# One batch's output stored during the last attention, and two products first in the last output projection

## The chip, the cores and the metric

The kernel runs on one core of a Trainium2 chip. The metric is the time of one execution on the device in microseconds; where several runs are shown, their median counts. All data are float32 in memory. The engines are named PE (matrix products), DVE (VectorE), ACT (ScalarE), POOL (GpSimd) and SP (here it only issues DMAs). Each engine works through its own queue in order.

## The reference

Two blocks follow each other, each a group normalisation, an attention and an addition to the block's input. The input is 8 images of 32 x 32 positions and 512 channels, so 1024 tokens in each of 8 batches.

```python
def reference(x, w_qkv, w_proj, b_proj, Wq, Wk, Wv, Wo, pos_emb_w, pos_emb_h):
    # layer 0: 16 heads of 32
    x = x + attention(_gn(x); w_qkv) @ w_proj + b_proj
    # layer 1: 4 heads of 128
    q = _gn(x) @ Wq / sqrt(128); k = _gn(x) @ Wk; v = _gn(x) @ Wv
    scores = q @ k + relative_logits(q, pos_emb_w, pos_emb_h)
    x = x + softmax(scores) @ v @ Wo
    return x
```

Here `_gn` is a group normalisation over 32 groups of channels; heads, reshapes and the form of the relative logits are cut.

## The kernel before, in words

**Layout.** A batch's activations lie transposed in SBUF: channels on the 128 partitions, in four chunks, and the 1024 tokens along the free dimension. Such a tensor is a `block` of 128 x 4 x 1024; eight of them are there (`BLOCKS`).

**Products.** All projections go through `seven`, a product of 2 x 2 blocks done in seven half-size products in place of eight. The moving operand is split into four quarters by chunk (`:HC`, `HC:`) and by token half (`:NB`, `NB:`). `forms` makes three sums (`s1`, `s2`, `s4`) of them and replaces the quarter `a21` by `a11 - a21`: four additions on DVE of 128 x 1024 elements. The seven moving operands are numbered 0 to 6: 0 is `a11`, 1 is `a12`, 2 is `s4`, 3 is `a22`, 4 is `s1`, 5 is `s2`, 6 is the new `a21`. Operands 0 and 1 are parts of the tensor itself, of its first token half. `ORDER` says in which order they are multiplied. Three banks of PSUM (`x`, `y`, `z`, from a ring of three) take the sums. A snapshot `p1` of bank `x` is taken by ACT after product 0; `a` and `b` are bank `y` plus `p1`, taken by DVE before more is added to the bank, so PE has to wait for them; `p7` is a snapshot of `z` by ACT. A projection consists of two units (`u` = 0 and 1) of 128 output columns of each half.

One product is eight matmul instructions of 32 columns (`by_columns`), four groups of columns side by side; the profile shows two records for each instruction, so `x16`.

**Weights.** `Stream` loads the weight parts in the order of the whole program's `plan`: after each product it issues the load that is seven products ahead, as a DMA on SP's queue, into a ring of 16 buffers (tag `w`).

**Output projection.** `after_1(b)` fetches the batch's saved activations from memory into a block `x2T`, runs `forms` on the attention's output (earlier, by a hook, in most batches), and then the two units. Results are added to `x2T` by the class `Onto`: `gather` adds snapshots on POOL, `add` adds banks on DVE. After each finished 128 x 512 part `add` calls `put_out`: a transpose on DVE into a tile `ot` (tag `row`, a ring of three), and four DMAs of 64 KB to the output, in pieces of 128 bytes. They are issued on SP; in the last batch every second one on ACT.

**The second attention.** `attention_1` has 4 heads x 2 query halves x 8 key tiles = 64 steps. A step multiplies scores on PE, takes the exponential on ACT into `e` (a ring of three), multiplies `e` with the values on PE, and adds `e` to a running sum `esum` on DVE. After eight steps `finish` and `normalise` divide by the sum: PE, ACT, DVE and, at the end, one multiplication on POOL.

**Order of the work.** The loop over `b` weaves the parts of three batches by generators and counts of steps. A scheduler of the framework then places the instructions in each engine's queue, mostly in the order of the program text; `issue_after` ties an instruction behind another one. In the last pass (`b` = 8) no first attention is left. The pass is the first output projection of batch 7, the second output projection of batch 6 (`after_1(6)`) with the normalisation of batch 7 woven in, the projections of batch 7 (`second`), and its attention. Behind the loop stands

```python
    run(after_1(B - 1, states[B - 1]))
```

and after it a check of all sums: `worst`, `bad`, a matmul `pf`, and `flag`, which every engine loads and branches on.

Of the kernel before, what the change touches and what calls it, by code (L numbers as in the profile page):

```python
# [17 lines left out]
P = 128  # L18
# [9 lines left out]
def quick_path(  # L28
# [52 lines left out]
    def bank(name, shape=None):  # L81
        return psum.tile(shape or [P, NB], F32, tag="bank", name=name, bufs=3)
# [80 lines left out]


    ORDER = [0, 5, 1, 4, 6, 2, 3]

    class Stream:

# [2 lines left out]
        def __init__(self, plan):  # L171
            self.plan = plan
            self.tiles = {}
            self.at = -1
            for i in ORDER:
                self.load(0, i)

        def load(self, n, i):
            if n >= len(self.plan):
                return  # L180
            m, rows, u = self.plan[n]
            if rows and u == 1:
                self.tiles[n, i] = self.tiles[n - 1, i]
                return
            got = []
            src = m.factor(i)
            if m.kept:
                got = [src[:, c, :] if rows else src[:, c, u * P : (u + 1) * P] for c in range(HC)]
                if i == ORDER[-1] and (u == 1 or rows):
                    m.kept = None  # L190
            elif rows:
                for c in range(HC):
                    t = mem.tile([P, HN], F32, tag="w", name=f"w_{m.name}_{n}_{i}_{c}", bufs=16)
                    nc.sync.dma_start(t, src[:, c, :])
                    got.append(t)
            else:
                t = mem.tile([P, HC, P], F32, tag="w", name=f"w_{m.name}_{n}_{i}", bufs=16)
                nc.sync.dma_start(t, src[:, :, u * P : (u + 1) * P])
                got = [t[:, c, :] for c in range(HC)]
            self.tiles[n, i] = got  # L200

        def unit(self, m, rows, u):
            self.at += 1
            assert self.plan[self.at] == (m, rows, u)
# [5 lines left out]
        def ahead(self, i):  # L210
            self.load(self.at + 1, i)

    def put_away(xT, name):
        kept = []
# [88 lines left out]

    in_place = [False]

    half_done = [None]

    def by_columns(out, weights, moving, start, stop, open_sum=False):
# [32 lines left out]
    def seven(fs, u, rows, sink, name, hook=None):  # L341

        def product(out, i, start):
            w, f = stream.take(i), fs[i]
            if not rows:
                for c in range(HC):
                    by_columns(out, w[c], f[:, c, :], start and c == 0, c == HC - 1, True)  # L350
            else:
                for t in range(2):
                    for c in range(HC):
                        by_columns(
                            out[:, t * HN : (t + 1) * HN],
                            f[:, c, (2 * u + t) * P : (2 * u + t + 1) * P],
                            w[c],
                            start and c == 0 and t == 0,
                            c == HC - 1,
                            True,  # L360
                        )
            stream.ahead(i)
# [9 lines left out]
        nc.vector.tensor_add(a, y, p1)  # L372
# [12 lines left out]
        p7 = snapshot("e1", f"p7_{name}")  # L385
        nc.scalar.copy(p7, z)  # L386
        yield HC
        product(y, 2, False)
        sink.c12(y, p1)
        if hook is not None:  # L390
            hook()
        yield HC
        product(z, 3, False)
        sink.c21(z, a)
        sink.c22(b, p7)
        yield HC

    class Plain:

# [237 lines left out]
    def attention_1(q, k, v, posT, b):  # L637

        steps = [(h, c, j) for h in range(H1) for c in range(NH) for j in range(NT)]
        state = {}  # L640

        def front(h, c, j):
            name = f"1_{b}_{h}_{c}_{j}"
            ps = bank(f"ps_{name}")
            keys = slice(j * P, (j + 1) * P)
            queries = slice(c * NB, (c + 1) * NB)
            nc.tensor.matmul(ps, k[h][:, keys], q[:, h, queries], start=True, stop=False)  # L647
            nc.tensor.matmul(ps, sel_flat[:, keys], posT[:, h, queries], start=False, stop=True)  # L648
            e = mem.tile([P, NB], F32, tag="e1", name=f"e_{name}", bufs=3)
            nc.scalar.activation(e, ps, AF.Exp, scale=1.0 / math.sqrt(D1))  # L650
            return e

        def back(h, c, j, e):
            name = f"1_{b}_{h}_{c}_{j}"
            if j == 0:
                state["acc"] = bank(f"acc_{name}")
                state["first"] = e
            acc = state["acc"]
            nc.tensor.matmul(  # L659
                acc,  # L660
                v[:, j, h * D1 : (h + 1) * D1],
                e,
                start=(j == 0),
                stop=(j == NT - 1),
            )
            if j == 1:
                state["esum"] = mem.tile([P, NB], F32, tag="es1", name=f"es_{name}", bufs=2)
                nc.vector.tensor_add(state["esum"], state["first"], e)  # L668
            elif j > 1:
                nc.vector.tensor_add(state["esum"], state["esum"], e)  # L670
            if j < NT - 1:
                return
            nc.scalar.copy(q[:, h, c * NB : (c + 1) * NB], acc)
            state["ended"] = (h, c, state["esum"])

        def finish(h, c, esum):
            name = f"1_{b}_{h}_{c}"
            su = bank(f"sums_{name}")
            nc.tensor.matmul(su, ones, esum, start=True, stop=True)
            normalise(q[:, h, c * NB : (c + 1) * NB], su, name)  # L680

        pending = None
        for at in steps:
            e = front(*at)
            ended = state.pop("ended", None)
            if pending is not None:
                back(*pending)
            pending = (*at, e)
            if ended is not None:
# [133 lines left out]

    def after_1(b, st, hook=None):

        if "ao1" not in st:
            forms_1(b, st)
        fs = st.pop("ao1")
        xT = fetch(st["kept"], block(f"x2T_{b}"))
        for u in range(2):  # L830

            def put_out(n, h):
                m = n * HC + u
                ot = mem.tile([P, NB], F32, tag="row", name=f"ot_{b}_{m}_{h}", bufs=3)
                nc.vector.transpose(ot, xT[m][:, h * NB : (h + 1) * NB])
                ot = ot.rearrange("p (t i) -> p t i", i=32)
                for a in range(P // 32):

                    queue = nc.scalar if b == B - 1 and a % 2 else nc.sync
                    queue.dma_start(  # L840
                        by_blocks(of[b, h * NB : (h + 1) * NB, :], m * P + 32 * a),
                        ot[32 * a : 32 * a + 32],
                    )

            stream.unit(WO, False, u)
            yield from seven(
                fs, u, False, Onto(halves(xT, u), then=put_out), f"wo_{b}_{u}", hook if u else None
            )

    def woven(main, side, start, gap, places=(0,)):  # L850

# [45 lines left out]
    WP, WQ1, WK1 = Matrix(w_proj, 0, "p"), Matrix(Wq, 0, "q1"), Matrix(Wk, 0, "k1")  # L897
    WV1, WO = Matrix(Wv, 0, "v1"), Matrix(Wo, 0, "o")
    def units(m, rows=False):
        return [(m, rows, u) for u in range(2)]  # L900

    FIRST = units(WQ0) + units(WK0) + units(WV0, True)
    plan = units(WV0, True) + [(m, False, u) for u in range(2) for m in (WQ0, WK0)]
    for b in range(B + 1):
        if b >= 1:
            plan += units(WP)
# [3 lines left out]
            plan += units(WQ1) + units(WK1) + units(WV1, True)  # L910
        if b + 1 < B:
            plan += FIRST
    plan += units(WO)

    states = [{} for _ in range(B)]
    load_first(states[0])
# [19 lines left out]
    for b in range(B + 1):  # L936
# [11 lines left out]
        if last is not None:  # L948
# [12 lines left out]
            if here is not None and coming is None:  # L961
# [5 lines left out]
                    H1 * NH * NT,  # L967
                )
                total += H1 * NT
            rest.append(woven(attention, incoming, 4, 6))  # L970
        else:
            rest.append(woven(rest_of_first(here), incoming, 0, 2))
# [503 lines left out]
```

## Time and profile before

| what | value |
|---|---|
| median of 5 runs | 3889.31 us (3886.48 to 3891.76) |
| profiled execution, its own time | 3885.46 us |
| its span, first to last instruction | 3883.7 us |
| PE busy | 3803.0 us, 98% |
| DVE busy | 2513.5 us, 65% |
| ACT busy | 1724.3 us, 44% |
| POOL busy | 620.4 us, 16% |
| granted PE clock, mean | 0.995 |
| second output projection of batch 6, first product | 3596.6 us from the start |
| attention of batch 7, first scores | 3711.3 us |
| last output projection, first product | 3843.0 us |
| last DVE instruction (a transpose of outputs) ends | 3875.7 us |

All places in the text are microseconds from the start of the span. A row of the timeline gives start, length, engine, line, operation, output and inputs with partitions x elements, and how many instructions are merged; in brackets stands the engine's idle time before it and what ended it. `SPq` and `ACTq` rows are DMA issues on those queues. The `p`, `f_ao` or `w_q` of a row are the program's tile names without numbers.

### The profile page before, as it was taken

The numbers are of one execution on the slowest core, as the hardware profiler recorded it, in microseconds if no ns is written. First come the engines' busy times: TensorE is split into PE (matmuls) and PEld (weight loads), VectorE is DVE, ScalarE is ACT, GpSimd is POOL, SyncE is SP. The second block draws the span as 40 slices with busy tenths as digits, with TensorE's granted clock in tenths as the row PEclk, the third lists the DMA queues.
The fourth block names the chain that finished last, engine by engine and source line by source line (L and its number), as shares of the span: only waits on it lengthen the run. The fifth ranks groups of instructions, "written<-read, shape, count | busy, mean of one in ns | idle before, by whom it ended". The sixth has DMA issues, their size and how long they took to land.

```text
span 3883.7 us, 79819 instructions
## 1 busy us (share of the span) xinstructions
PE 3803.0 (98%) x34478; PEld 1368.3 (35%) x34478; DVE 2513.5 (65%) x2905; ACT 1724.3 (44%) x1767; POOL 620.4 (16%) x400
## 2 busy tenths in 40 slices
PE   8999899999999999999999999999999999999998
PEld 3222244232442224432344323433234332334353
DVE  5777675576745867458674686646866568665544
ACT  2554553445434454344543445444453445553132
POOL 1341001121101210112100121111211112001101
PEclk9999999999999999999999999999999999999999
DMA  5221120133201422023220231203411033111401
GB/s 170 80 104 55 36 63 1 39 117 71 60 3 55 114 60 55 9 88 85 51 55 15 92 91 38 52 20 97 89 40 41 25 97 76 33 45 32 122 18 23
DMA packets 482984, 234.73 MB, mean 60 GB/s; under 512 B 269600, under 2 KB 461376, under 8 KB 481600
## 3 DMA queue, kind: packets, MB, share of 16 engines
q1 hardware_dynamic: 470992, 213.74, 20.4%
q0 software_dynamic: 2608, 13.70, 1.0%
q8 instruction: 274, 4.49, 0.5%
q10 hardware_dynamic: 9024, 2.10, 0.3%
q14 instruction: 86, 0.70, 0.1%
HBM read 170.72 MB, written 58.72 MB: 59 GB/s over the span
## 4 chain that ended last, share of the span: by engine, by line
PE 86%; DVE 8%; ACT 3%; issue 2%; POOL 1%; DMA 1%; SPq 0%; DVEq 0%; POOLq 0%; ACTq 0%
PE ps L532 12%; PE ps L647 11%; PE acc L659 11%; PE acc L551 10%; PE y_k L312 4%; PE y_v L312 4%; PE y_q L312 4%; PE ps L648 3%; PE x_k L312 3%; PE z_k L312 3%; PE x_v L312 3%; PE x_q L312 3%; PE z_v L312 3%; PE z_q L312 3%; ACT e L540 2%; DVE es L562 2%
## 5 line engine op out<-in xcount | busy, mean ns | idle before, releaser
L540 ACT ACTIVATE e<-ps 128x2048 f32<-128x2048 f32 x512 | 961.6, 1878 | 836.8 <-PE ps L532 621.8
L562 DVE TENSOR_TENSOR es<-es,e 128x2048 f32<-128x2048 f32 x384 | 889.6, 2317 | 421.7 <-ACT e L540 419.0
L532 PE MATMUL ps<-q,k 32*64 32x512 f32 x8192 | 575.5, 613 | 27.9 <-ACT e L540 27.9
L650 ACT ACTIVATE e<-ps 128x512 f32<-128x512 f32 x512 | 305.7, 597 | 572.6 <-PE ps L648 539.2
L551 PE MATMUL acc<-e,v 128*32 128x512 f32 x4096 | 547.3, 606 | 0.0
L647 PE MATMUL ps<-q,k 128*128 128x512 f32 x1024 | 525.0, 594 | 0.3 <-DVE posT L633 0.3
L659 PE MATMUL acc<-e,v 128*128 128x512 f32 x1024 | 521.9, 592 | 0.0
L517 POOL TENSOR_TENSOR q<-q,su 128x512 f32<-128x512 f32 x128 | 213.4, 1667 | 1592.0 <-DVE su L513 1547.2
L670 DVE TENSOR_TENSOR es<-es,e 128x512 f32<-128x512 f32 x384 | 290.7, 757 | 251.0 <-ACT e L650 248.9
L648 PE MATMUL ps<-posT,sel 128*128 128x512 f32 x512 | 406.7, 794 | 0.0
L647 PEld LDWEIGHTS ps<-q,k 128*128 128x128 f32 x1024 | 192.5, 190 | 251.2 <-issue 244.8
L532 PEld LDWEIGHTS ps<-q,k 32*64 32x64 f32 x8192 | 120.1, 130 | 421.8 <-issue 219.3
L659 PEld LDWEIGHTS acc<-e,v 128*128 128x128 f32 x1024 | 193.1, 189 | 146.8 <-issue 105.2
L551 PEld LDWEIGHTS acc<-e,v 128*32 128x32 f32 x4096 | 81.5, 108 | 411.9 <-issue 365.1
L560 DVE TENSOR_TENSOR es<-e,e 128x2048 f32<-128x2048 f32 x64 | 174.8, 2731 | 36.9 <-ACT e L540 36.9
L497 DVE STREAM_TRANSPOSE tu<-su 128x512 f32<-128x512 f32 x128 | 90.5, 707 | 127.5 <-ACT su L495 127.4
L648 PEld LDWEIGHTS ps<-posT,sel 128*128 128x128 f32 x512 | 97.3, 190 | 122.5 <-issue 122.5
L495 ACT COPY su<-sums 128x512 f32<-128x512 f32 x128 | 74.9, 585 | 146.4 <-PE sums L572 78.5
L633 DVE TENSOR_TENSOR posT<-pp,posT 32x512 fp32r<-32x512 f32 x128 | 112.0, 875 | 31.9 <-ACT posT L628 30.6
L668 DVE TENSOR_TENSOR es<-e,e 128x512 f32<-128x512 f32 x64 | 44.2, 690 | 134.8 <-ACT e L650 134.8
L421 POOL TENSOR_TENSOR k<-b_k,p_k 128x512 f32<-128x512 f32 x32 | 51.1, 1598 | 479.7 <-ACT p_k L386 479.7
L628 ACT CAST posT<-pp 32x512 fp32r<-32x512 f32 x128 | 105.8, 826 | 45.6 <-PE pp L615 44.5
(195 smaller groups left out, 4451.1 us busy)
## 6 DMA issues: line engine op xcount, KB each, us to landing
w_qkv<-ws_qkv SPq DMA_DIRECT2D x168, 128.0 KB, 2.5
d<-x0T SPq DMA_DIRECT2D x32, 512.0 KB, 3.4
x1T<-d SPq DMA_DIRECT2D x32, 512.0 KB, 6.0
d<-x1T SPq DMA_DIRECT2D x32, 512.0 KB, 3.6
x2T<-d SPq DMA_DIRECT2D x32, 512.0 KB, 6.3
w_qkv<-in_L_conv_w_qkv SPq DMA_DIRECT2D x126, 128.0 KB, 2.2
out<-ot SPq DMA_DIRECT2D x240, 64.0 KB, 2.0
xs<-in_x SPq DMA_DIRECT2D x224, 64.0 KB, 2.5
```

The lines of the kernel that those rows point to most:

```text
L312: ins = nc.tensor.matmul(out[columns, :], weights[:, columns], moving, start=start, stop=stop, skip_group_check=open_sum,)
L517: nc.gpsimd.tensor_tensor(dst, dst, su, op=ALU.mult)
L532: nc.tensor.matmul(ps[some, r, :], k[m][rows, j * P + 64 * i : j * P + 64 * i + 64], q[m][rows, h * NB : (h + 1) * NB], start=True, stop=True,
L540: nc.scalar.activation(e, ps, AF.Exp, scale=D0 ** -0.5)
L551: nc.tensor.matmul(acc[r * D0 : (r + 1) * D0, :], v[:, j, c0 : c0 + D0], e[:, r, :], start=(j == 0), stop=(j == NT - 1),)
L560: nc.vector.tensor_add(state["esum"], state["first"], e)
L562: nc.vector.tensor_add(state["esum"], state["esum"], e)
L647: nc.tensor.matmul(ps, k[h][:, keys], q[:, h, queries], start=True, stop=False)
L648: nc.tensor.matmul(ps, sel_flat[:, keys], posT[:, h, queries], start=False, stop=True)
L650: nc.scalar.activation(e, ps, AF.Exp, scale=1.0 / math.sqrt(D1))
L659: nc.tensor.matmul(acc, v[:, j, h * D1 : (h + 1) * D1], e, start=(j == 0), stop=(j == NT - 1),)
L670: nc.vector.tensor_add(state["esum"], state["esum"], e)
```

## The change

Two edits, with the stream's order adapted to the second.

1. For batch 6 (`b == B - 2`) `put_out` no longer transposes and stores a finished part. It only notes it down. The last attention is woven with `late_output`, which does one of the eight noted parts from step 4 on and then in each sixth step; each transpose is tied behind the newest addition to the attention's sum (`issue_after(added[0])`).
2. The last output projection is written out in `after_last`. Products 0 and 1 of both units come first (`two_first`), with the forms made after them, and then the five other products of each unit (`five_last`). The plan of weights follows: two parts for each unit, then five.

```diff
-    run(after_1(B - 1, states[B - 1]))
+    after_last(B - 1, states[B - 1])
...
+            if here is None:
+                incoming = later(late_output, past)
             rest.append(woven(attention, incoming, 4, 6))
...
-    plan += units(WO)
+    plan += [(WO, False, u, some) for some in (FIRST_TWO, LAST_FIVE) for u in range(2)]
...
+    FIRST_TWO, LAST_FIVE = [0, 1], [5, 4, 6, 2, 3]
...
             elif j > 1:
-                nc.vector.tensor_add(state["esum"], state["esum"], e)
+                added[0] = nc.vector.tensor_add(state["esum"], state["esum"], e)
...
+    def two_first(fs, u, sink, name):
+
+        product = taken(fs, u, False)
+        x = bank(f"x_{name}")
+        product(x, 0, True)
+        p1 = snapshot("e1", f"p1_{name}")
+        nc.scalar.copy(p1, x)
+        product(x, 1, False)
+        sink.c11(x)
+        return p1
+
+    def five_last(fs, u, sink, name, p1):
+        product = taken(fs, u, False)
+        y = bank(f"y_{name}")
+        product(y, 5, True)
+        a = snapshot("es1", f"a_{name}")
+        nc.vector.tensor_add(a, y, p1)
+        sink.early(p1, a)
+        product(y, 4, False)
+        b = snapshot("es1", f"b_{name}")
+        nc.vector.tensor_add(b, y, p1)
+        sink.middle(b)
+        z = bank(f"z_{name}")
+        product(z, 6, True)
+        p7 = snapshot("e1", f"p7_{name}")
+        nc.scalar.copy(p7, z)
+        product(y, 2, False)
+        sink.c12(y, p1)
+        product(z, 3, False)
+        sink.c21(z, a)
+        sink.c22(b, p7)
...
+    def put_out(b, st, xT, u):
+        def put(n, h):
+            m = n * HC + u
+            ot = mem.tile([P, NB], F32, tag="row", name=f"ot_{b}_{m}_{h}", bufs=3)
+            late = b == B - 2
+            with tc.issue_after(added[0].ins) if late else nullcontext():
+                nc.vector.transpose(ot, xT[m][:, h * NB : (h + 1) * NB])
...
+        def put_later(n, h):
+            st.setdefault("late", []).append(lambda: put(n, h))
+
+        return put_later if b == B - 2 else put
+
+    def late_output(st):
+
+        for put in st.pop("late"):
+            put()
+            yield 0
+
+    def after_last(b, st):
+
+        x = st["ao"]
+        xT = fetch(st["kept"], block(f"x2T_{b}"))
+        sinks = [Onto(halves(xT, u), then=put_out(b, st, xT, u)) for u in range(2)]
+        early = [x[:, :HC, :NB], x[:, HC:, :NB]]
+        p1s = []
+        for u in range(2):
+            stream.unit(WO, False, u)
+            p1s.append(two_first(early, u, sinks[u], f"wo_{b}_{u}"))
+        fs = forms(x, f"ao1_{b}")
+        for u in range(2):
+            stream.unit(WO, False, u)
+            five_last(fs, u, sinks[u], f"wo_{b}_{u}", p1s[u])
```

The rest of the diff moves the inner function of `seven` that multiplies one operand into a function of its own (`taken`), and lets `Stream` count its loads one by one along the plan in place of unit by unit.

More of the change, by code (lines that the diff above doesn't have):

```diff
@@ L174, in __init__ @@
             self.at = -1
-            for i in ORDER:
-                self.load(0, i)
+            self.uses = iter([(n, i) for n, (_, _, _, some) in enumerate(plan) for i in some])
+            for _ in ORDER:
+                self.ahead()
         def load(self, n, i):
[L179 to L182, printed above, removed]
+            m, rows, u, some = self.plan[n]
+            if rows and u == 1 and not m.kept:
                 self.tiles[n, i] = self.tiles[n - 1, i]
@@ L188, in load @@
                 got = [src[:, c, :] if rows else src[:, c, u * P : (u + 1) * P] for c in range(HC)]
-                if i == ORDER[-1] and (u == 1 or rows):
+                if i == some[-1] and u == 1:
                     m.kept = None
@@ L203, in unit @@
             self.at += 1
-            assert self.plan[self.at] == (m, rows, u)
+            assert self.plan[self.at][:3] == (m, rows, u)
         def take(self, i):
@@ L208, in take, with ahead @@
             return got
-        def ahead(self, i):
-            self.load(self.at + 1, i)
+        def ahead(self):
+            use = next(self.uses, None)
+            if use is not None:
+                self.load(*use)
     def put_away(xT, name):
@@ L304, in quick_path @@
     in_place = [False]
+    added = [None]
     half_done = [None]
@@ L339, in snapshot, with taken @@
         return mem.tile([P, NB], F32, tag=tag, name=name, bufs=3 if tag == "e1" else 2)
-    def seven(fs, u, rows, sink, name, hook=None):
+    def taken(fs, u, rows):
         def product(out, i, start):
@@ L361, in product, with seven @@
                         )
-            stream.ahead(i)
+            stream.ahead()
+        return product
+    def seven(fs, u, rows, sink, name, hook=None):
+        product = taken(fs, u, rows)
         x = bank(f"x_{name}")
@@ L824, in after_1 @@
     def after_1(b, st, hook=None):
-        if "ao1" not in st:
-            forms_1(b, st)
         fs = st.pop("ao1")
@@ L830, in after_1 @@
         for u in range(2):
[L832 to L843, printed above, removed]
@@ L845, in after_1 @@
             stream.unit(WO, False, u)
             yield from seven(
-                fs, u, False, Onto(halves(xT, u), then=put_out), f"wo_{b}_{u}", hook if u else None
-            )
+                fs, u, False, Onto(halves(xT, u), then=put_out(b, st, xT, u)), f"wo_{b}_{u}",
+                hook if u else None,
+            )
+    def put_out(b, st, xT, u):
[5 more added lines that the diff above has]
+                nc.vector.transpose(ot, xT[m][:, h * NB : (h + 1) * NB])
+            ot = ot.rearrange("p (t i) -> p t i", i=32)
+            for a in range(P // 32):
+                queue = nc.scalar if b == B - 1 and a % 2 else nc.sync
+                queue.dma_start(
+                    by_blocks(of[b, h * NB : (h + 1) * NB, :], m * P + 32 * a),
+                    ot[32 * a : 32 * a + 32],
+                )
+        def put_later(n, h):
+            st.setdefault("late", []).append(lambda: put(n, h))
+        return put_later if b == B - 2 else put
@@ L899, in units @@
     def units(m, rows=False):
-        return [(m, rows, u) for u in range(2)]
+        return [(m, rows, u, ORDER) for u in range(2)]
     FIRST = units(WQ0) + units(WK0) + units(WV0, True)
-    plan = units(WV0, True) + [(m, False, u) for u in range(2) for m in (WQ0, WK0)]
+    plan = units(WV0, True) + [(m, False, u, ORDER) for u in range(2) for m in (WQ0, WK0)]
     for b in range(B + 1):
```

## The prediction

> **What bounds the kernel now.** The head of the page and the chain that ended last say that TensorE (PE) is the bound: it is busy for 98% of the span, and 86% of the chain lies on it.
>
> ```profile
> PE 3803.0 (98%) x34478; PEld 1368.3 (35%) x34478; DVE 2513.5 (65%) x2905; ACT 1724.3 (44%) x1767; POOL 620.4 (16%) x400
> PE 86%; DVE 8%; ACT 3%; issue 2%; POOL 1%; DMA 1%; SPq 0%; DVEq 0%; POOLq 0%; ACTq 0%
> ```
>
> So only idle time of PE, or slow time on it, can be won, and only where the change reaches. The built programs' queues differ in two places alone: in the output projection of batch 6 with the first products of batch 7's queries behind it, and after the last attention. I read the timeline of both. First place (start, length, engine, line; in brackets the idle time before and what ended it):
>
> ```profile
> 3604.94 18.98 SPq L840 DMA_DIRECT2D out<-ot  x20
> 3613.88 1.90 PE L312 MATMUL x_wo<-q,w_o 128*32 128x512 f32 x16
> 3616.18 0.70 DVE L835 STREAM_TRANSPOSE ot<-x2T 128x512 f32<-128x512 f32 x1
> 3617.51 1.92 PE L312 MATMUL y_wo<-f_ao,w_o 128*32 128x512 f32 x16 [1.74 <-DVE a_wo L372]
> ...
> 3632.86 4.14 SPq L840 DMA_DIRECT2D out<-ot  x8
> 3634.70 1.90 PE L312 MATMUL z_q<-x1T,w_q 128*32 128x512 f32 x16
> 3637.09 0.46 SPq L198 DMA_DIRECT2D w_q<-in_L_conv_Wq  x1
> 3639.56 2.77 PE L312 MATMUL x_q<-x1T,w_q 128*32 128x512 f32 x16 [2.96 <-DMA w_q<-in_L_conv_Wq]
> 3642.03 2.87 PE L312 MATMUL y_q<-f_xn,w_q 128*32 128x512 f32 x16
> 3644.68 1.93 PE L312 MATMUL x_q<-x1T,w_q 128*32 128x512 f32 x16
> ```
>
> PE stands still twice. At 3617.51 it waits for VectorE's (DVE) snapshot `a_wo`, which came behind three transposes of outputs. At 3639.56 it waits for a weight whose load went out at 3637.09, right behind eight stores of outputs on SP's queue. Then two products run at half speed. The table by stretches confirms it (columns: length, busy time of PE, PEld, DVE, ACT, POOL, then the granted clock):
>
> ```profile
> 3640.50:3644.00 3.50, 3.50 (x24) 1.16 (x20) 0.00 (x0) 0.58 (x1) 0.00 (x0) 0.51 0.89 243
> ```
>
> Second place, the tail:
>
> ```profile
> 3843.02 1.92 PE L312 MATMUL x_wo<-q,w_o 128*32 128x512 f32 x16
> 3845.70 1.93 PE L312 MATMUL x_wo<-q,w_o 128*32 128x512 f32 x16 [0.75 <-issue]
> 3847.09 1.27 POOL L431 TENSOR_TENSOR x2T<-x2T,p_wo 128x512 f32<-128x512 f32 x1
> 3847.17 2.27 DVE L332 TENSOR_TENSOR f_ao<-q 128x1024 f32<-128x1024 f32 x1 [1.10 <-POOL q L517]
> 3849.48 1.23 DVE L333 TENSOR_TENSOR f_ao<-f_ao,q 128x1024 f32<-128x1024 f32 x1
> 3850.76 1.92 PE L312 MATMUL y_wo<-f_ao,w_o 128*32 128x512 f32 x16 [3.14 <-DVE f_ao L333]
> ```
>
> Two products need no sums and run at once; then PE waits 3.14 us for the second sum.
>
> [...] one stretch of 3.4 us at 0.51 follows a gap of 2.96 us, while the 3.14 us of the tail brought none. [...] L332 takes 2.27 us beside POOL's L431, against 1.21 us at 3592.30. [...]
>
> **Part 1: batch 6's outputs leave the projection.** Eight transposes (0.70 us each, 5.6 us of DVE) and 32 stores on SP (median 0.50 us each to issue, 16 us) move to the last attention. A product's rhythm on PE is 1.72 us, from start to start.
> - The second snapshot. Without transposes DVE runs: normalisation 2 until 3612.67, 3 until 3613.39, an addition until 3614.0, normalisation 4 (which POOL's addition holds up until about 3614.65) until 3615.2, snapshot until 3615.8. PE starts at 3615.88 instead of 3617.51: 1.63 us won. Bounds: 0, if DVE is no earlier, and 1.91, the whole delay against 3613.88 + 1.72.
> - The weight. It and the loads ahead of it now wait only for PE to free their buffers, long before 3636. PE goes on at 3634.70 + 1.72 = 3636.42 instead of 3639.56: 3.14 us. Bounds 0 and 3.14.
> - The half clock. From 3639.56 to 3644.68 are 5.12 us for two products that take 3.44: 1.68 us. Bounds 0 (another gap calls it up) and 1.68.
> - Next late: the product `y_q` wants the bank that the addition to `x2T` frees. By the rows' lengths DVE frees it at about 3624.4, and PE wants it at 3624.49. No margin, but a miss costs some tenths; I take 0.1 off.
>
> Sum: 1.63 + 3.14 + 1.68 - 0.1 = 6.35 us.
> - What the moved work meets. In the attention a step takes 1.95 us, of which DVE works 0.69 on the sum and idles 1.25. One transpose each six steps fits in. If it delays a sum, three buffers of `e` give slack: the exponential at 3789.21 shares its buffer with that at 3795.05, and its sum is done at 3790.53, 4.5 us earlier. SP has nothing to issue between 3709.8 and 3854.9, and a tile's buffer returns after three more tiles (35 us), against 3.3 us for the slowest landing. `x2T` of batch 6 lives longer, in one of eight blocks of which six are then in use, and batch 7's load takes another one. Cost 0; without the cover 8 x 0.71 = 5.7 us.
>
> **Part 2: the tail.** No product is added or dropped. PE's built queue is now: product 0 of block 0, one matmul of product 0 of block 1, product 1 of block 0, the other seven of product 0 of block 1, then one matmul of `y_wo` of block 0, which needs the second sum, and only behind it product 1 of block 1. So one product of the two slips into the gap; PE idles from about 3849.1 to 3850.76. The fourth early product comes after it, at full use. On DVE four operations now stand ahead of block 0's snapshot: two additions (0.68 each), a transpose (0.71), and POOL's second early addition (1.27), which holds up the third sum. With the rows' lengths: second sum 3850.71, POOL until 3851.96, third sum 3853.05, transpose 3853.7, fourth 3854.9, addition 3855.5, snapshot 3856.15. PE has done block 1's product, the rest of `y_wo` and five matmuls of `z_wo` by then and waits some 0.3 to 1.1 us, a stall that is new. From 3856.2 follow `y_wo`'s second product, then waits for the snapshots `b_wo` (0.7 us each, partly filled, as now) and six more products: `y_wo`'s last one ends at 3870.05, against about 3871.9 now. The third last output tile is transposed by 3871.5 instead of 3872.69 + 0.71 = 3873.40: 1.9 us won. The last three tiles (0.79 MB) leave at some 135 GB/s by the DMA view of the tail, so stores run without a break to the end and the end follows that tile. On ACT's queue block 1's copy `p_wo`, now held behind stores until 3864.88, moves ahead of them; PE lost 0.2 us there. The flag's chain moves ahead of the last products: its matmul (0.38) hides in the wait for `b_wo`, and SP's load of the flag[...] between two tiles' stores that lie 2 us apart.
>
> Bounds: at the low end the new stall and a half-speed window (1.7) eat all, 0; at the high end the whole 3.14 us. I take 1.9, since the same working applied to the kernel before gives its starts within 0.1 us.
>
> **Sum.** 6.35 + 1.9 = 8.25 us. The profiled execution took 3885.46 us (span 3883.7 and 1.8 around it), so it would take 3877.2. The median of the runs, 3889.31, lies 3.85 above; the same saving gives 3881.1 us, 0.21% less.
>
> **Rivals.**
> 1. The tail gives nothing: third sum and snapshot come later than worked out[...]. For it: POOL's 1.27 us already lengthened L332. Against: the sums above hold it. 3889.31 - 6.35 = 3883.0.
> 2. The weight wait stays: something else on SP's queue, say the loads that follow, is late. For it: SP's queue is in order and waits for PE's buffers. Against: the load's buffer is free after `y_wo`, about 3609. Then 1.63 + 1.9 - 0.1 = 3.4 us, 3885.9.
> 3. More than the sum: the median run is 3.85 us slower than the profiled one, which two more half-speed windows (1.68 each) would about make. If they come from the tail's 3.14 us gap and the 1.7 us gaps, they go too: 3889.31 - 8.25 - 3.4 = 3877.7.
> 4. Slower: the moved stores stand on SP behind the weight loads for the last projection. If these get their buffers only late in the attention, the fourth transpose, some 35 us after the first (about 3720), waits for a tile buffer, and DVE's queue, the sums and PE stand with it, a microsecond for each. It decides from 3755 on; to end 7.8 us slower, the loads must be held until 3755 + 8.25 + 7.8 = 3771, giving 3897. Against it: now they all are out by 3709.8, before the attention's first scores at 3711.30.
>
> **How the numbers follow.** 0.2% (7.8 us) is about what a measurement of this kernel can tell from no change. Forecast 55%, 3880 to 3883, a bare half of it past the bound of 3881.5; rival 1 13%; rival 2 7%; rival 3 21%; rival 4 4%. Faster by over 0.2%: 0.55 x 0.62 + 0.21 and a little of rival 1, about 0.57; slower 0.03; within 0.2% the rest, 0.40. The range takes in rivals 1 and 3 and most of rival 2: 3877.0 to 3886.0.
>
> **What would show it.** Right: no wait of PE for `w_q` and one, not two, for `a_wo` before the last queries; granted clock 1.00 there; no transpose before the last attention; its 64 steps as long as now; a gap of some 1.6 us before the first `y_wo` in the tail and a short new one before the second. Wrong: transposes that lengthen steps of the attention, a gap of 3 us left in the tail, or a half-speed stretch at another place.

## Result and profile after

| | before | after |
|---|---|---|
| median | 3888.01 us (45 runs, 3886.01 to 3892.65) | 3878.48 us (25 runs, 3876.58 to 3883.82) |
| profiled execution, its own time | 3885.46 us | 3884.55 us |

The ratio of the times is 0.9976, with a 95% interval of 0.9971 to 0.9982: 9.3 us less, between 7.0 and 11.3. The prediction said 8.25 us less, from a median of 3889.31 that five runs had given.

The two profiled executions differ by 0.9 us only. That is no contradiction, but they can't be compared as wholes. In the profile after, batch 7's first output projection (`x_wp`) starts at 3579.85, before at 3572.53, and nothing in the instructions ahead of it differs. So everything below is measured from that start: 311.17 us to the end of the span before, 302.85 us after, 8.32 us less. (The expectations quoted below say 311.10 and 302.78, from a start read 0.07 us later.) The end of the span is printed to 0.1 us only, so tails and totals here and below are good to about 0.05 us. The stretch splits at marks that both kernels have:

| stretch | before | after | difference | predicted |
|---|---|---|---|---|
| A: `x_wp` to the first scores of the last attention | 138.77 | 132.16 | -6.61 | -6.35 |
| the last attention, to the first product of the last projection | 131.72 | 131.73 | 0.0 | 0 |
| tail: from there to the end of the span | 40.68 | 38.96 | -1.72 | -1.9 |

The head of the page and its chain after look as they did, which shows how little such shares say of a change of 0.2%:

```profile
PE 3806.4 (98%) x34478; PEld 1367.7 (35%) x34478; DVE 2516.7 (65%) x2905; ACT 1725.3 (44%) x1767; POOL 619.6 (16%) x400
PE 86%; DVE 8%; ACT 3%; issue 2%; POOL 1%; DMA 0%; SPq 0%; DVEq 0%; POOLq 0%; ACTq 0%
```

The waits of PE over the changed stretch (engine, line, what it waited for: us in total, times, longest) do show it. There is no wait for `w_q` any more, one for `a_wo` in place of two, and 1.4 us for the second sum in the tail in place of 3.1. The longest ones, first before and then after:

```profile
PE y_wo L312 <- DVE a_wo L372: 3.4, 2, 1.7
PE y_wo L312 <- DVE f_ao L333: 3.1, 1, 3.1
PE x_q L312 <- DMA w_q<-in_L_conv_Wq: 3.0, 1, 3.0
```

```profile
PE y_wo L316 <- DVE a_wo L380: 1.6, 1, 1.6
PE y_wo L316 <- DVE f_ao L337: 1.4, 1, 1.4
```

Timeline after, batch 6's second unit and the first queries:

```profile
3621.20 1.90 PE L316 MATMUL x_wo<-q,w_o 128*32 128x512 f32 x16
3622.32 0.68 DVE L380 TENSOR_TENSOR a_wo<-y_wo,p_wo 128x512 f32<-128x512 f32 x1
3623.05 1.92 PE L316 MATMUL y_wo<-f_ao,w_o 128*32 128x512 f32 x16
...
3640.25 1.90 PE L316 MATMUL z_q<-x1T,w_q 128*32 128x512 f32 x16
3641.96 1.90 PE L316 MATMUL x_q<-x1T,w_q 128*32 128x512 f32 x16
3643.68 1.90 PE L316 MATMUL y_q<-f_xn,w_q 128*32 128x512 f32 x16
3645.40 1.90 PE L316 MATMUL x_q<-x1T,w_q 128*32 128x512 f32 x16
```

From start to start the three places are 1.85 us (3.63 before), 1.71 (4.86) and 3.44 for two products (5.12). The differences, 1.78, 3.15 and 1.68 us, are the whole 6.61 of stretch A. SP issues the loads of the keys' weights from 3628.47 on, 13 us before `x_q` starts. The stretch table gives full clock there (last three columns: granted clock, DMA share, GB/s):

```profile
3641.00:3645.00 4.00, 4.00 (x44) 1.20 (x40) 0.88 (x2) 0.59 (x1) 0.00 (x0) 1.00 0.23 67
```

The tail, first the third last transpose of outputs before, then rows of after:

```profile
3872.69 0.71 DVE L835 STREAM_TRANSPOSE ot<-x2T 128x512 f32<-128x512 f32 x1
```

```profile
3843.74 6.32 PE L316 MATMUL x_wo<-q,w_o 128*32 128x512 f32 x48
3847.89 2.29 DVE L336 TENSOR_TENSOR f_ao<-q 128x1024 f32<-128x1024 f32 x1 [1.10 <-POOL q L557]
3850.21 1.22 DVE L337 TENSOR_TENSOR f_ao<-f_ao,q 128x1024 f32<-128x1024 f32 x1
3851.49 0.62 PE L316 MATMUL y_wo<-f_ao,w_o 128*32 128x512 f32 x1 [1.43 <-DVE f_ao L337]
...
3854.95 1.88 PE L316 MATMUL z_wo<-q,w_o 128*32 128x512 f32 x10
3855.92 0.67 DVE L422 TENSOR_TENSOR a_wo<-y_wo,p_wo 128x512 f32<-128x512 f32 x1
3856.65 2.33 PE L316 MATMUL y_wo<-f_ao,w_o 128*32 128x512 f32 x17
...
3871.69 0.71 DVE L881 STREAM_TRANSPOSE ot<-x2T 128x512 f32<-128x512 f32 x1
```

Three products stand ahead of the gap in place of two. The next stall is the one behind `z_wo x10`: ten matmuls at 1.72/16 us fill 1.07 of the 1.70 us to the next start, and PE goes on as soon as `a_wo` is there. The third last output tile (the last row) is transposed 28.66 us after the first `x_wo`, against 30.38 before. That is 1.72 us, and the span's end, 10.3 us later in both, moves with it.

### The profile page after: what moved, and what is told of

Read it like the earlier page. It is cut to its first block, busy times and chain, and to the rows that moved or that the text cites. A ratio compares the mean times of both kernels' runs of the same rounds, so it can differ in the third digit from the quotient of the medians.

```text
span 3882.7 us, 79818 instructions
## 1 busy us (share of the span) xinstructions
PE 3806.4 (98%) x34478; PEld 1367.7 (35%) x34478; DVE 2516.7 (65%) x2905; ACT 1725.3 (44%) x1767; POOL 619.6 (16%) x400
## 4 chain that ended last, share of the span: by engine, by line
PE 86%; DVE 8%; ACT 3%; issue 2%; POOL 1%; DMA 0%; SPq 0%; DVEq 0%; POOLq 0%; ACTq 0%
PE ps L572 12%; PE ps L687 11%; PE acc L699 11%; PE acc L591 10%; PE y_k L316 4%; PE y_v L316 4%; PE y_q L316 4%; PE ps L688 3%; PE x_k L316 3%; PE x_v L316 3%; PE x_q L316 3%; PE z_k L316 3%; PE z_v L316 3%; PE z_q L316 3%; ACT e L580 2%; DVE es L602 2%
```

## Experiments

All of them are read from the start of `x_wp` too. The table has every profile (us).

| kernel | `x_wp` starts | A | attention | tail | A to end | timed, ratio to before |
|---|---|---|---|---|---|---|
| before | 3572.53 | 138.77 | 131.72 | 40.68 | 311.17 | |
| before, second | 3574.54 | 137.03 | 131.72 | 42.91 | 311.66 | |
| before, third | 3574.49 | 138.95 | 131.72 | 41.04 | 311.71 | |
| after | 3579.85 | 132.16 | 131.73 | 38.96 | 302.85 | 0.9976 (0.9971 to 0.9982) |
| after, second | 3574.39 | 132.22 | 131.73 | 39.16 | 303.11 | |
| e1, late outputs alone | 3579.29 | 132.20 | 131.73 | 40.78 | 304.71 | 0.9983 (0.9977 to 0.9990) |
| e2, new tail alone | 3573.90 | 137.20 | 131.73 | 38.87 | 307.80 | 0.9988 (0.9981 to 0.9995) |
| e3, no stores | 3573.04 | 134.78 | 131.72 | 40.66 | 307.16 | |
| e4, no transposes | 3572.62 | 132.26 | 131.73 | 41.09 | 305.08 | |
| e5, outputs bunched | 3577.29 | 132.07 | 131.73 | 39.21 | 303.01 | |
| e6, four products in order | 3576.72 | 132.04 | 131.73 | 40.31 | 304.08 | 0.9979 (0.9971 to 0.9987) |
| e7, other tail | 3572.84 | 132.14 | 131.73 | 37.79 | 301.66 | 0.9975 (0.9966 to 0.9983) |
| e8, e7 with three waits removed | 3576.36 | 132.13 | 131.72 | 34.99 | 298.84 | 0.9966 (0.9952 to 0.9979) |
| e8, second | 3575.14 | 132.26 | 131.73 | 35.27 | 299.26 | 0.9966 (0.9954 to 0.9978) |

### The two parts, each alone (e1, e2)

```diff
 # e1: after, with the last projection as before
-    plan += [(WO, False, u, some) for some in (FIRST_TWO, LAST_FIVE) for u in range(2)]
+    plan += units(WO)
...
-    after_last(B - 1, states[B - 1])
+    forms_1(B - 1, states[B - 1])
+    run(after_1(B - 1, states[B - 1]))
 # e2: after, with batch 6's outputs put at once
-            late = b == B - 2
+            late = False
...
-        return put_later if b == B - 2 else put
+        return put
...
-            if here is None:
-                incoming = later(late_output, past)
```

> The late outputs alone; the last projection as before. Measured from the first product of batch 7's x_wp, where nothing has changed yet, to the end of the span (311.10 us before, 302.78 after): theory of two separate parts: 304.5, that is 6.6 less, no wait of PE for w_q, one for a_wo, and the tail from the first x_wo to the end of the span 40.7 as before. Timed: 6.6 us less, ratio 0.9983. Rival, that the tail needs the late outputs or gives the larger part: a gain under 4 us here.

> The new last projection alone; batch 6's outputs stored at once, as before. Theory of two separate parts: from the first x_wo to the end of the span 39.0 us (40.68 before, 38.96 after), so 1.7 us less; ratio 0.9996, which a timing can hardly tell from 1. The waits for w_q (some 3 us) and twice for a_wo are as before. If a gap of 3 us calls up the half clock in every run, two x_q products take 5.1 us[...]. Rival: the whole gain is part 1's and the tail stays at 40.7.

Measured: e1 is 6.46 us shorter than before, 6.57 of it in A, with the tail as before, and 0.9983 in time. e2's tail is 1.81 us shorter and its two waits for `a_wo` are there (3.4 us together). 6.57 and 1.81 make 8.38, after's 8.32 within the reading. So the parts are independent, and each is worth what its place shows. One thing in e2 was left open by its expectation: the gap before `x_q` is there, 2.94 us, but the half clock is not: the granted clock was 1.00 from 3640.90 to 3644.30. Timeline of e2:

```profile
3640.92 1.92 PE L316 MATMUL x_q<-x1T,w_q 128*32 128x512 f32 x16 [2.94 <-DMA w_q<-in_L_conv_Wq]
3642.63 1.93 PE L316 MATMUL y_q<-f_xn,w_q 128*32 128x512 f32 x16
3644.35 1.93 PE L316 MATMUL x_q<-x1T,w_q 128*32 128x512 f32 x16
```

The timed gain of e2, 4.7 us (1.9 to 7.4), lies above the 1.7 expected. The next section gives a reason for part of the excess. The first 415 us of the program, which take some us more in one execution than in another (last experiment; after's two profiles start `x_wp` at 3579.85 and 3574.39), can add to it either way; how often they did in the timed runs isn't known.

### When the half clock came (before twice more)

> The kernel before once more, unchanged. In two profiles a gap of 2.9 us ahead of x_q was followed once by the half clock and once not. [...] a gap of about 3 us again[...]. If the start of x_wp is set by half-speed windows in the first 415 us: 3572.7 with seven of them and about 2.3 us more for each one above.

> The kernel before a third time, with the same expectation as the second: the gap of about 3 us stays, and the half clock follows it or not[...].

"Half clock" is a stretch in which PE was granted 0.5 of its clock. The gap before `x_q` came both times, 2.97 and 2.95 us. In the second profile no half clock followed it (the products `x_q` and `y_q` took 1.92 and 1.93 us), but one followed the gap of 3.13 us in the tail. In the third it followed `x_q`'s gap (the granted clock was 0.51 from 3642.70 to 3646.10). Tail of the second profile, and its stretch table at that place:

```profile
3851.03 3.29 PE L312 MATMUL y_wo<-f_ao,w_o 128*32 128x512 f32 x16 [3.13 <-DVE f_ao L333]
```

```profile
3851.40:3854.80 3.40, 3.40 (x20) 0.87 (x16) 2.20 (x3) 0.00 (x0) 0.00 (x0) 0.51 0.00 0
```

The same for every gap of about 3 us in these two places, with the product that stood behind it:

| gap, kernel | its length | the product behind it took | half clock next |
|---|---|---|---|
| tail, before second | 3.13 | 3.29 | yes |
| `x_q`, before | 2.96 | 2.77 | yes |
| `x_q`, before third | 2.95 | 2.57 | yes |
| tail, before | 3.14 | 1.92 | no |
| tail, before third | 3.14 | 1.92 | no |
| `x_q`, e2; tail, e3 | 2.94; 3.15 | 1.92; 1.92 | no |
| `x_q`, before second | 2.97 | 1.92 | no |
| tail, e1; tail, e4 | 3.14; 3.13 | 1.92; 1.92 | no |

Ten gaps, and the half clock came behind three. Their lengths do not tell them apart: 3.13 us had it in the second profile of before and not in e4, and 2.95 and 2.96 us had it where 2.94 and 2.97 had not. What else decides is not shown. The gaps of 1.4 to 1.7 us that both kernels have were followed by none in these profiles: the products behind those of 1.63 to 1.74 us took 1.92 or 1.93 us, and after, with 1.63 and 1.43 us, was granted 1.00 from 409.5 to 3877 us.

For the change this means that both removed gaps carried a chance of some 1.7 us (A is 138.77 and 138.95 us with it, 137.03 without), not a certainty: 3 of 10 here. Two such gaps make 1.0 us on average at that share, and 1.7 at that of the three profiles of before alone (3 of 6); both are estimates from these few gaps. e2 keeps the gap at `x_q` but has lost that of the tail, and with it its chance: by the same estimates 0.5 to 0.9 us more than 1.7, which lies inside e2's interval.

The expectation's second half fell. The second profile of before has nine half-speed stretches of 3.4 us in its first 415 us and starts `x_wp` at 3574.54, the third has seven and starts it at 3574.49. Their number alone does not set that start; the last experiment comes back to it.

### What held the weight (e3, e4)

```diff
 # e3: before, batch 6's part of the output not stored
-                for a in range(P // 32):
+                for a in range(P // 32 if b != B - 2 else 0):
 # e4: before, batch 6's tiles stored as they lie in x2T
...
-                nc.vector.transpose(ot, xT[m][:, h * NB : (h + 1) * NB])
+                if b == B - 2:
+                    ot = xT[m][:, h * NB : (h + 1) * NB]
+                else:
+                    nc.vector.transpose(ot, xT[m][:, h * NB : (h + 1) * NB])
```

> The kernel before without batch 6's 32 stores (that part of the output stays unwritten); its eight transposes stay where they were. If the w_q wait comes from stores on SP's queue: no wait for w_q, clock 1.00, x_wp to the first attention scores 138.70 - 3.14 - 1.68 = 133.9 us, and the second a_wo wait of 1.7 us stays. Rival, that the weight waits for something else (its buffer, the loads ahead of it): a gap of about 3 us stays before x_q.

> The kernel before without batch 6's eight transposes; the 32 stores stay, straight from x2T (that part of the output is in the wrong layout). If the second a_wo wait comes from transposes on DVE's queue: one a_wo wait instead of two, 1.6 us less there, and the w_q wait stays at some 3 us or grows to 4 to 5, since PE comes to it earlier and SP's stores take as long as before. Rival, that DVE is late for another reason[...]: the second a_wo wait stays above 1 us.

e3 came out in kind: no wait for `w_q`, full speed (`x_q` and `y_q` took 1.90 us each), and both waits for `a_wo` still there. Waits of PE in e3:

```profile
PE y_wo L312 <- DVE a_wo L372: 3.4, 2, 1.7
PE y_q L312 <- DVE a_q L372: 0.4, 1, 0.4
```

A is 134.78 us, not 133.9. Without stores the scheduler places two transposes ahead of the snapshot `a_q`, and `y_q` starts 2.34 us after the product before it in place of 1.72, 0.6 us lost. Most of the rest lies in the keys' products, 0.2 us, as much as two profiles of before differ by in A (138.77 and 138.95).

e4 did not come out as expected. The second `a_wo` wait went, as it should, but the wait for `w_q` went too, with all 32 stores still on SP. Three rows of the kernel before show why. DVE stands idle for 2.67 us, for PE's `y_q`, then makes the sum `b_q`, and only behind it come the last two transposes; their inputs had been ready since 3626.5 (the addition at 3625.81 takes 0.68):

```profile
3625.81 0.68 DVE L436 TENSOR_TENSOR x2T<-z_wo,x2T 128x512 f32<-128x512 f32 x1
3631.52 0.69 DVE L380 TENSOR_TENSOR b_q<-y_q,p_q 128x512 f32<-128x512 f32 x1 [2.67 <-PE y_q L312]
3632.13 1.29 DVE L835 STREAM_TRANSPOSE ot<-x2T 128x512 f32<-128x512 f32 x2
```

In e4 the same eight stores go within 1 us of the addition's end:

```profile
3625.27 0.68 DVE L436 TENSOR_TENSOR x2T<-z_wo,x2T 128x512 f32<-128x512 f32 x1
3626.86 5.42 SPq L844 DMA_DIRECT2D out<-x2T  x8
3632.37 0.45 SPq L198 DMA_DIRECT2D w_q<-in_L_conv_Wq  x1
3634.81 1.92 PE L312 MATMUL x_q<-x1T,w_q 128*32 128x512 f32 x16
```

The weight's load leaves 59.75 us after `x_wp`'s start, against 64.56 before, and the product comes 1.78 us after the one before it (3633.03), just in time: the load still goes out right behind the eighth store, so with the issue time of the stores alone PE comes out even, but with nothing to spare. What made SP late by those 3 us were stores that waited for transposes, which stood on DVE behind a sum that waited for PE. Either end of the chain can be taken away.

### Does the spread over the attention matter (e5)

```diff
-            rest.append(woven(attention, incoming, 4, 6))
+            rest.append(woven(attention, incoming, 4, 6 if here is not None else 1))
```

> The kernel after with the eight late outputs in eight steps on end of the last attention, instead of one each six steps. A step takes 1.95 us, its sum and a transpose take 1.4 us of DVE, four stores 2.0 us of SP. Theory, that DVE's idle 1.25 us a step covers a transpose: 131.7 us from the first scores to the first x_wo, as with the spread outputs, or up to 1 us more if buffers of tiles come back late. Rival, that the spread is what made it free: DVE stops for tile buffers (three, one store after another at some 0.5 us each) and the attention takes 3 us or more longer.

The attention takes 131.73 us again. All eight transposes now start within 33 us in place of 86, not quite in eight steps on end as expected (that would be 16 us): the first four lie within 8 us, the others 4 to 8 us apart (the tile's rows, first of e5, then of after: duration min/median/max in ns, first and last start):

```profile
L881 DVE STREAM_TRANSPOSE ot<-x2T x8: 698/704/705, 3716.9 to 3750.2; 128x512 f32<-128x512 f32 x8
```

```profile
L881 DVE STREAM_TRANSPOSE ot<-x2T x8: 698/705/705, 3719.6 to 3805.7; 128x512 f32<-128x512 f32 x8
```

DVE's idle time in each step covers them either way. It is the place that made them free, not the spacing of `after`; eight of them in eight steps were not run.

### The tail's next bound (e6, e7, e8)

```diff
 # e6: after, the matmuls of the early products and of y_wo's first kept in program order
-            if in_place[0]:
+            if in_place[0] or held[0]:
                 tc.keep_in_program_order(ins)
```

> The kernel after with all four early products ahead of the first y_wo on PE, where after has three and the fourth behind one matmul of y_wo. Theory, that DVE's queue sets the next stage (second sum, two additions, third sum, transpose, fourth sum, snapshot a_wo): the gap of 1.43 us before y_wo closes to under 0.4, PE waits about as much longer for the snapshot, and the tail (38.96 us from the first x_wo to the end of the span) stays within 0.3 us. Rival, that PE's split order cost the gap: 1.4 us less, 37.5.

Both were wrong in size: the tail is 40.31 us, 1.35 longer than after's. Waits of PE in e6's tail:

```profile
PE y_wo L317 <- DVE a_wo L424: 2.1, 1, 2.1
PE x_wo L317 <- issue: 0.8, 1, 0.8
PE x_wo L317 <- ACT p_wo L413: 0.7, 1, 0.7
```

The wait of 1.43 us for the sum is gone, and two waits for the copy of a first product before the second may be added to its bank stand in its place, 1.44 us together (the one put down to `issue` ends 0.1 us after the copy). DVE then sets the next stage: `a_wo` ends 13.58 us after the first `x_wo` (12.85 in after), behind one transpose more, and only two matmuls of `z_wo` stand ahead of the waiting one where after has ten. So PE's split order was no loss. That DVE's queue is what PE waits for here is in line with the theory, and e7 and e8 went on from it.

```diff
 # e7: after, the last projection's products in another order, x banks in a tile of four banks;
 # the code that puts them in this order is cut
-    FIRST_TWO, LAST_FIVE = [0, 1], [5, 4, 6, 2, 3]
+    LAST = [(0, 0), (1, 0), (0, 1), (1, 1), (0, 5), (0, 6), (0, 4), (1, 5), (0, 2), (0, 3), (1, 4), (1, 6), (1, 2), (1, 3)]
 # e8: e7, with
-        xs = [spare[:, u, :] for u in range(2)]
+        xs = [spare[:, 0, :], psum.tile([P, NB], F32, tag="acc", name="last_1", bufs=1)]
...
+            if held[0]:
+                self.gather(0, 1, a)
+                self.gather(1, 0, p1)
+                return
             self.gather(1, 0, p1)
             self.gather(0, 1, a)
...
-        sinks[0].c11(xs[0])
+        with tc.issue_after(first_sum[0].ins):
+            sinks[0].c11(xs[0])
```

(In `LAST` each pair is block and operand. `first_sum[0]` is the snapshot `a_wo` of block 0; `c11` of block 1 is tied to it in the same way, and POOL's additions keep the program's order.)

> The kernel after with another order of the last projection: four early products first, each into a bank of its own, the products of both blocks in turn, DVE's and POOL's additions to x2T only behind the sums and snapshots that PE waits for. In after PE is idle or waits for 28.87 - 14 x 1.717 = 4.8 us between the first x_wo and the last z_wo. Theory, that these waits are DVE's order: the last z_wo ends 25 us after the first x_wo and the span 1 to 4 us earlier than after's, where the additions moved behind now stand close ahead of the last tiles, so not all of it is kept. Rival, that the stores' drain (0.79 MB at some 135 GB/s) sets the end whatever PE does: the tail stays at 39 us.

> The kernel of e7 with three waits taken away: the first product of block 1 gets a bank of another tile, so it need not wait for the copy of block 0's (0.7 us in e7); POOL's first addition to x2T comes after the snapshot a_wo, so the sums of the quarters run without it (1.2 us each for 2.3 and 2.2); DVE's additions of the early products come after a_wo. Theory, that the sums and DVE's order are what PE waits for in e7: four early products end 7.1 us after the first x_wo, y_wo follows within 0.3 us and a_wo no longer stops PE; the last z_wo ends 24.6 us after the first x_wo (27.8 in e7, 28.9 in after) and the span at 34.7 to 36.5 (37.8 in e7). Timed: 2 to 4 us less than after, a ratio to before of about 0.997. Rival, that additions and transposes moved behind only come back at the end: the last tiles are transposed no earlier and the tail stays above 37 us.

> The kernel of e8 once more, unchanged, for more timed runs: theory, that its tail is 4 us shorter than after's in every execution: again a ratio to before of 0.9966, below after's 0.9976; the tail 35.0 us and the last z_wo 24.9 us after the first x_wo. Rival, that the first timing was lucky: a ratio of 0.9975 or more.

e7 gained 1.17 us in the tail, the low end, and its time can't be told from after's. The last `z_wo` ends 27.8 us after the first product, not the 25 expected. Its waits show what was left:

```profile
PE y_wo L317 <- DVE a_wo L928: 1.0, 1, 1.0
PE last L317 <- issue: 0.8, 1, 0.8
PE last L317 <- ACT p_wo L919: 0.7, 1, 0.7
```

In e8 these are gone. The four early products run without a break, the sums take 1.2 us each, and `a_wo` is ready 0.7 us before PE's next start (3849.83 against 3850.54):

```profile
3840.21 7.08 PE L317 MATMUL last<-q,w_o 128*32 128x512 f32 x64
3844.37 1.23 DVE L337 TENSOR_TENSOR f_ao<-q 128x1024 f32<-128x1024 f32 x1 [1.10 <-POOL q L564]
3845.63 1.23 DVE L338 TENSOR_TENSOR f_ao<-f_ao,q 128x1024 f32<-128x1024 f32 x1
3847.10 1.90 PE L317 MATMUL y_wo<-f_ao,w_o 128*32 128x512 f32 x16
3849.14 0.69 DVE L936 TENSOR_TENSOR a_wo<-y_wo,p_wo 128x512 f32<-128x512 f32 x1
3850.54 5.33 PE L317 MATMUL y_wo<-f_ao,w_o 128*32 128x512 f32 x48
```

The last `z_wo` (its tile is named `last` here) ends 24.93 us after the first product (28.87 in after; fourteen products alone are 24.0) and the tail takes 34.99 and 35.27 us in its two profiles, 4 us less than after's. Timed, both series gave 0.9966 to before. e8 is below after's 0.9976 as a middle value; the intervals overlap, so that it beats after rests on the tails of the profiles. e8 makes its three changes at once; how much each gives was not measured apart.

### The late start of the unchanged part (after once more)

> The kernel after once more, unchanged. If the late start of x_wp in its profile (3579.85, ten half-speed windows in the first 415 us, against 3572.53 and seven in the kernel before) is chance and not the change: x_wp may start anywhere from 3572.5 to 3580, in step with the number of windows, and 302.8 us follow up to the end. Rival, that something in the changed kernel delays the first part: 3579 to 3580 again.

`x_wp` starts at 3574.39 in it and the rest takes 303.11 us. So the late start of the first profile does not belong to the changed kernel as such; its two profiles are 5.5 us apart there. This profile has seven half-speed stretches of 3.4 us in the first 415 us, the first had ten, but as the kernel before showed, the count alone does not settle it.

The traces show a second reason. From 485 us on all fourteen profiles keep step with the first one of before up to `x_wp`, within 0.3 us; the spread arises ahead of that. At about 210 us DVE adds to a sum of the first attention while POOL adds up weights (`prep_v`). In the first profile of after DVE starts 0.22 us before a POOL addition and takes 6.13 us, and PE then waits 2.34 us for the sum `b_k` behind it; in the second profile of the same kernel DVE starts while POOL's addition is running, takes 2.94 us, and PE does not wait. First profile, then second:

```profile
210.84 6.13 DVE L602 TENSOR_TENSOR es<-es,e 128x2048 f32<-128x2048 f32 x1 [1.46 <-ACT e L580]
211.06 3.75 POOL L146 TENSOR_TENSOR prep_v<-prep_v 128x512 f32<-128x512 f32 x3
217.62 0.62 PE L316 MATMUL y_k<-f_xn,w_qkv 128*32 128x512 f32 x1 [2.34 <-DVE b_k L388]
```

```profile
209.35 7.28 POOL L146 TENSOR_TENSOR prep_v<-prep_v 128x512 f32<-128x512 f32 x3
211.30 2.94 DVE L602 TENSOR_TENSOR es<-es,e 128x2048 f32<-128x2048 f32 x1 [0.34 <-ACT e L580]
```

Five profiles have the long form (6.13 or 6.14 us: after, e1, e5, e6, e8), and they are the five that start `x_wp` last, at 3576.36 to 3579.85. The nine with the short form (2.93 to 2.95 us) start it at 3572.53 to 3575.14. Which form comes differs between executions of one kernel (after, e8). All five are of kernels built on after, none of the five profiles built on before has it, so this count does not exclude that the change makes it more frequent. Against that, the timed gain, 9.3 us, is not below the 8.3 between the marks, as it would be if after started late more often. What sets the nine others up to 2.6 us apart stays open.

## Why the prediction came out as it did

- **The second `a_wo` wait** was worked out by moving DVE's remaining rows up: 1.63 us. It measured 1.78 (3.63 - 1.85), in its bounds, and e4, which only takes the transposes away, confirms the cause.
- **The weight**, 3.14 us: measured 3.15 (4.86 - 1.71). The cause was named too shortly. "Right behind eight stores of outputs on SP's queue" is true, but e4 kept these stores on SP and had no wait. They were late because their transposes were. Moving both away was right for either reason.
- **The half clock**, 1.68 us: true of the profile it was read from (5.12 - 3.44), but taken for certain. Of three profiles of before, one had none there, and one had it in the tail, where the prediction counted nothing. On average the two removed gaps are worth an estimated 1.0 to 1.7 us by the section on it, where the sum has 1.68, so that this term fits is in part luck. Rival 3 put two further half-speed stretches of a median run at the tail's gap and at the gaps of 1.7 us. The first of these brought one in 1 of 6 profiles with that gap, the others brought none. What rival 3 started from, the median above the profile, has mainly another reason: the second and third profile of before took 3888.0 us, about the median, and 2.0 of the 2.5 us that they took beyond the first lie ahead of `x_wp`.
- **The bank of `y_q`**, 0.1 us lost: there was no loss; `y_q` follows 1.71 us after `x_q`.
- **The attention**, 0: measured 0.0, with spread (after) and bunched outputs (e5). Rival 4, moved stores held on SP, did not come: the attention took 131.73 us, 131.72 before.
- **The tail**, 1.9 us: 1.72. The working held step by step: the gap before the first `y_wo` 1.43 us (some 1.6 said), the snapshot `a_wo` 12.85 us after the first `x_wo` (13.13), the third sum 1.71 us beside a POOL addition of 1.80 us, a new short stall of 0.6 us (0.3 to 1.1), `y_wo`'s last product ending 27.15 us after it (27.03). Rival 1, that the tail gives nothing, fell by e2.
- **The weight wait stays** (rival 2) fell with the waits of after.
- **The total.** 8.25 us said, 8.32 and 8.06 in the profiles by the same marks, 9.3 (7.0 to 11.3) timed. The predicted 3881.1 lies 2.6 us above the median of 3878.48: 1.3 of it is the starting median, 3889.31 of five runs against 3888.01 of 45; the rest is within the interval of the saving. Term by term the waits were right. That the total came so near also rests on the half clock, which the profile that was read had once in its two gaps, by chance near the average (0.6 to 1.0 times by those estimates).

## What to carry to other kernels

A long list of stores on a queue need not be what delays the load behind it (here, with the stores ready in time, PE came out even); look for the store whose input is late, and follow that back through the other engines. Sum a change's parts within marks that both profiles share, since here the untouched first part of one kernel differed by 5.5 us between two executions, more than half of the whole gain. Look there for a place where two engines start within a fraction of a us of each other (0.22 us in after's first profile). Where a gap of PE is followed by half clock, count that time with the share of such gaps that had it (3 of 10 here); and where PE waits for sums, keep POOL's additions and DVE's work on finished results behind them, as e8 does (1.23 us a sum, 2.27 and 2.19 in e7).

## What the runs showed of the hardware

- Of ten gaps of PE of 2.94 to 3.15 us three were followed by the half clock (2.96, 3.13 and 2.95 us, one in each profile of before; granted clock 0.51 over 3.4 us), and the product behind them took 2.57 to 3.29 us. Seven, of 2.94 to 3.15 us, were not, and it took 1.92 us.
- The same first part of the program took 3572.5 to 3579.9 us in fourteen profiles. Half-speed stretches of 3.4 us in its first 415 us, seven to ten in the profiles of before and after, go along with this only loosely. A DVE addition of 128 x 2048 near 210 us that took 6.13 us beside three POOL additions in five profiles, and 2.94 us in nine, tells the five latest starts from the others.
- Two sums of 128 x 1024 on DVE took 1.23 us each in e8, with no addition of POOL beside them, and 2.27 and 2.19 us in e7 with two POOL additions from 3840.78 on.
